# The order of the transfer queue where a quantised GLU kernel passes from its first batch to its second

## The chip, the cores and the metric

The kernel runs on one core of a Trainium2 chip. The metric is device microseconds (us) of one execution; less is better. The kernel before was timed in three runs: median 718.24 us, from 718.19 to 719.2.

## The reference

Four batches of 1024 tokens with 512 features go through one gated layer. The up weights are 4096 x 512, the down weights 512 x 2048.

```python
scale = cond @ norm_w.T + 1.0
h = x * (scale[:, None, :] * jax.lax.rsqrt(mean(x * x, axis=-1) + EPS))
val, gate = jnp.split(h @ up_w.T, 2, axis=-1)
h = val * jax.nn.gelu(gate, approximate=False)
hq = round(h * 127 / max|h|) / (127 / max|h|)             # per token
wq = clip(round(down_w / mean|down_w|), -1, 1) * mean|down_w|
y = hq @ wq.T + x
```

So `down_w` is reduced to a mean and to one of -1, 0, 1 per weight. The change concerns the transfers that bring `down_w` for that second step.

## The kernel before

**Tiles and slots.** The 2048 features of the value and of the gate are cut into 16 blocks of 128 (`NJ`). A batch has two halves of 512 tokens. One block of one batch is a slot, numbered g = 16 b + j; batch b = 1, the second, begins with slot 16. A slot multiplies by Winograd's scheme, with 7 products instead of 8. A product (`product`, L696) is 6 matmuls of 128 x 128 by 128 x 512 in fp16, in three terms of high and low parts. In the first batch only blocks 9 to 15 go that way; the earlier ones are done plainly (L711).

**Order in a slot.** `slot(g, ...)` writes this row on TensorE (PE), with PSUM banks A, B and E: `first` of g (bank A), `fourth` of g (E), `second` of g (B), `third` of the slot before (A of that slot), `fifth` of g (A), `gate` of the slot before (E), `value` of g (A). ScalarE (ACT) copies the bank between: `first_copy` (L803), `fourth_copy` (L811), `fifth_copy` (L818, it has to be done before `value` accumulates on the same bank), and it computes the two Gelus (L825, L842). VectorE (DVE) makes the sums and outputs.

**Weights.** A block has seven sums of its quarter weights, split in high and low fp16, at places 0 to 6 of a buffer in `SXY` or `S_more`. They are made in the first batch, written out to `s_dram` (`s_spill`, L469) and read back for the later batches (`s_load`): `s_load_x(g)` brings places 5 and 6 by a plain transfer (L485) and places 0 to 2 by a transposing one (L483), `s_load_y(g)` brings place 4 (L485) and place 3 (L483). `first` and `second` read places 5 and 6, `fourth`, `fifth` and `value` places 0, 1 and 2, and `gate` and `third` places 3 and 4. Slots 16 and 17 use the two blocks that are still on the core (`KEPT` = 2). Slot 18 is the first that needs loads, into the second buffer of `SXY`, which block 13 had. In slot j of the second batch `loads()` issues `s_load_x` for two slots ahead and `s_load_y` for one ahead.

**The signs of `down_w`.** They are made in eight parts n = 0 to 7 of 128 x 1024. `d_fetch(n)` (L542) loads a part, 512 KB, into one of three buffers by n modulo 3 (tags `xn`, `xt`, `nx`). On ACT `d_round(n)` (L546) and `d_sign(n)` (L553) turn it into signs in fp8, two parts to a tile `tn`. `d_turn(m)` (L556) is a transposing transfer of such a pair, m = 0 to 3, into `wd`. Fetch n + 3 needs `d_sign(n)` done; `d_turn(m)` needs `d_sign(2 m + 1)`. `D_LATE` places the ACT steps: parts 0 and 1 in slot 16, 2 and 3 in slot 17, 4 in slot 18, 5 and 6 in slot 19, 7 in slot 20. They are put between the Gelu at L825 and `fifth_copy`, or behind `fifth_copy`. DVE first reads `wd` in slot 25, at 258.2 us.

**The queue.** All these transfers are issued by SyncE (SP) in the order in which the code is written. SP carries out each row's waits before it goes on, so a row that waits holds up all rows behind it. The framework gives the transfers eight completion semaphores in turn: a row also waits until the transfer eight places ahead of it has landed. The string `FIRST_BATCH` is the written-out order of the first batch up to the last slots, and `D_MOVES` says which fetches and turns are issued in which slot j of the second batch. Before, they are passed to `s_load_x` as `between`, and so stand between its L485 and its L483.

Of the kernel before, what the change touches and what calls it, by code (L numbers as in the profile page):

```python
# [51 lines left out]
def glu_quant_kernel(  # L52
# [121 lines left out]
    def po_bank(name, shape=None):  # L174
        return bank("po", 3, shape, name)
# [313 lines left out]
    def s_load_x(g, between=()):  # L489
        s_load(g, *LOADS[0])  # L490
        for f in between:
            f()
        s_load(g, *LOADS[1])
# [15 lines left out]
    def d_at(n):  # L509

        return n // 4 + 2 * (n % 2), n // 2 % 2, n % 2
# [26 lines left out]
    def d_fetch(n):  # L538

        v = wpool.tile([P, HF], F32, name=f"dn_{n}", tag=("xn", "xt", "nx")[n % 3], bufs=1)  # L540
        c, u, _ = d_at(n)
        SP.dma_start(out=v, in_=down_w[c * P : (c + 1) * P, u * HF : (u + 1) * HF])  # L542
        dn[n] = v
# [189 lines left out]
    def gains(b):  # L733
        sg[b] = sm.tile([P, NJ, 2], F32, name=f"sg_{b}", tag="sg")
        DVE.tensor_scalar(sg[b], sw, dx[:, b : b + 1], None, ALU.mult)
# [509 lines left out]
    def second_part():  # L1245
# [18 lines left out]
        ((3, "y"), d_round, 6), ((3, "y"), d_sign, 6), ((4, "x"), d_round, 7), ((4, "x"), d_sign, 7),  # L1264
    ]
    D_MOVES = {
        0: ((d_turn, 0), (d_fetch, 3), (d_fetch, 4)), 1: ((d_turn, 1), (d_fetch, 5), (d_fetch, 6)),
        3: ((d_turn, 2), (d_fetch, 7)), 4: ((d_turn, 3),),
    }
    def second_slot():  # L1270
        w_turn(1)
        w_high(1)
        first_scale(4, ACT)
        first_scale(5, DVE)
        w_low(1)
# [80 lines left out]
    def take(steps):  # L1356
# [68 lines left out]
        gains slot.15.0 t_sum.3.0 s_spill.14.2 t_high.3.1 t_sum.3.1 slot.15.1 s_turn.15.0 s_high.15.1 t_low.3.0  # L1425
        t_turn.3.0 t_low.3.1 t_sum.3.2.1 s_low.15.1 max.5.1.1 slot.14.13 t_sum.3.3.1 t_high.3.2 t_turn.3.1
        slot.15.6 slot.14.14 s_spill.15.0 slot.14.8 s_turn.15.1 slot.15.7 t_low.3.2 slot.14.9 t_turn.3.2
        s_spill.13.1 slot.15.4 d_fetch.0 s_spill.15.2 slot.13.15 slot.14.11 slot.15.5 s_spill.8.2 max.6.1.0
        max.6.1.1 d_fetch.1 max.6.0.0 s_spill.6.2 max.6.0.1 d_fetch.2 slot.15.2 slot.15.3 slot.15.13 slot.14.12
        slot.15.14 s_spill.15.1 s_spill.14.1 slot.14.15  # L1430
    """

# [92 lines left out]
    for b in range(1, B):  # L1525
        dve, act = Filler(), Filler()
        if b > 1:
            gains(b)
        am = am_tile(b - 1)
        dq = state[b - 1] = sm.tile([P, 2 * NA], F32, name=f"dq_{b}", tag="dq")  # L1530
        if b == 1:
            for at, f, n in D_LATE:
                act.add(at, 1.1, lambda now, f=f, n=n: f(n))
        last_pair = NJ // 2 - 1
        for h in range(2):
            add_pair(
                dve, act, b - 1, last_pair, h, (0, "xz"[h]),
                lambda now, h=h: token_max(b - 1, h, am),
            )
        for h in range(2):  # L1540
            for cost, f in token_scale(h, am):
                dve.add((1, "x"), cost, lambda now, f=f: f())
        add_pieces(dve, act, b - 1, am, PIECES, (2, "x"))
        for i in range(NJ // 2 - 1):
            for h in range(2):
                add_pair(dve, act, b, i, h, (2 * i + 3, "x"))
        steps = {}
        pairs = {}
        if b + 1 < B:
            sc = []  # L1550
            steps[3, "z"] = [(lambda b=b, sc=sc: sc.append(cond_load_scale(b + 1)), (0, 0))]
            steps[5, "z"] = [(lambda b=b, sc=sc: cond_bring(b + 1, sc[0]), (0.4, 0))]
            p0 = b * NJ + 12
            plan = [
                (None, p0, ((6, "z"), (7, "x"), (7, "y"), (9, "y"), (10, "x"), (10, "z"))),
                (p0 + 4, None, ((9, "y"), (10, "x"), (10, "y"), (11, "y"), (12, "x"), (12, "x"))),
                (None, None, ((10, "y"), (11, "x"), (11, "y"), (13, "x"), (13, "y"), (13, "z"))),
                (p0 + 2, p0 + 4, ((9, "z"), (12, "x"), (12, "y"), (14, "x"), (14, "y"), (14, "z"))),
            ]
            for a, (at, nx_at, places) in enumerate(plan):  # L1560
                def make(a=a, at=at, nx_at=nx_at, b=b):
                    toks[a] = Tokens(b + 1, a, at, nx_at)
                    toks[a].load()
                fs = [
                    make,
                    lambda a=a: toks[a].norm(),
                    lambda a=a, sc=sc: toks[a].scale_and_sum(sc[0]),
                    lambda a=a: toks[a].high(),
                    lambda a=a: toks[a].low(DVE),
                    lambda a=a: toks[a].turn(),  # L1570
                ]
                costs = ((0, 0), (0, 1.6), (0, 1.5), (0, 2.1), (2.6, 0), (0, 0))
                for place, f, c in zip(places, fs, costs):
                    steps.setdefault(place, []).append((f, c))
        for j in range(NJ):
            g = b * NJ + j
            down = b + 1 < B and j in DOWN
            if down:
                pair, a = pairs[j], DOWN[j]
                xrs = [down_load(b - 1, h, a) for h in range(2)]  # L1580
            early_sums, late_sums = D_SUM_AT.get((b, j), ((), ()))
            left = SLOT_US + PAIR_US * down - OWN_US + 0.4
            more = D_SUM_US * len(late_sums) + 0.7 * (j + 1 == min(DOWN) and b + 1 < B)
            left -= D_SUM_US * len(early_sums) + more
            if b + 1 < B:
                left -= KEPT_US.get(j, 0)
            mine = {p: [sum(c[e] for _, c in steps.get((j, p), ())) for e in range(2)] for p in "xyz"}
            left -= sum(mine[p][0] for p in "xyz")
            act_left = {"x": 2.7, "y": 2.2 if down or b == 1 and j in (0, 1, 3, 4, 5, 6) else 1.1, "z": 0}

            def run(p):
                nonlocal left
                for f, _ in steps.get((j, p), ()):
                    f()
                if p == "x":
                    cap = min(left, 3.9 - 1.2 * (j in (1, 2)) - mine["x"][0] - (0 if down else mine["y"][0] + more))
                    left -= cap - dve.run((j, p), cap)
                elif p == "z":
                    left = dve.run((j, p), left)
                if p != "z":  # L1600
                    act.run((j, p), act_left[p] - mine[p][1])

            def early():
                if down:
                    pair.first([po_bank(f"po_{b}_{a}_{n}") for n in range(3)])
                    pair.sums(None, h_slots(g)[:, 0, 1])
                d_sums(early_sums)

            def next_pair():
                if b + 1 < B and j + 1 in DOWN:  # L1610
                    pairs[j + 1] = Pair(b - 1, DOWN[j + 1])
                    pairs[j + 1].sum1(h_slots(g + 1)[:, 0, 0])

            def more_sums():
                next_pair()
                d_sums(late_sums)

            mid = [nothing] * 3
            if j + 1 == min(DOWN):
                mid[0] = more_sums  # L1620
            if down:
                mid = [
                    lambda: (next_pair(), pair.third(xrs, dq), d_sums(late_sums)),
                    pair.fourth,
                    lambda: (loads(), pair.fifth()),
                ]

            def loads():
                if NJ + KEPT <= g + 2 < B * NJ:
                    moves = D_MOVES.get(j, ()) if b == 1 else ()  # L1630
                    s_load_x(
                        g + 2, [lambda f=f, n=n: f(n) for f, n in moves]
                    )
                if NJ + KEPT <= g + 1 < B * NJ:
                    s_load_y(g + 1)


            if b + 1 == B and j in DOWN and DOWN[j] < 3:
                pairs[DOWN[j]] = Pair(b - 1, DOWN[j])
                places = old_places(DOWN[j])  # L1640
                pairs[DOWN[j]].sum1(places[0])
                pairs[DOWN[j]].sums(*places[1:])
            if j == 4:
                token_turn(b - 1, am)
            if j == 5:
                bring_dq = token_undo(b - 1, dq)
            if j == 6:
                bring_dq()
            if j == NJ - 1:
                get_ready()  # L1650
            elif b == 1 and j == 0:
                get_ready()
            slot(g, lambda: run("x"), lambda: run("y"), lambda: run("z"), early, mid)
            if not down:
                loads()
        assert not act.items and not dve.items, (b, dve.items, act.items)


    b = B - 1
# [165 lines left out]
```

## Time and profile before

| what | value |
|---|---|
| median of three runs | 718.24 us (718.19 to 719.2) |
| the profiled execution's own time | 718.03 us |
| its span, first to last instruction | 716.1 us |
| PE busy in the span | 708.5 us (99%) |
| DVE, ACT, POOL busy | 590.4, 427.8, 144.9 us |
| granted TensorE clock | 0.999 |

Rows of the timeline give the start, the duration, the engine, the line, the operation and its tiles, and in square brackets how long the engine had been idle ahead of it and what ended that. Several instructions of a line are merged into one row. A matmul's end is modelled and overlaps the next start by about 0.17 us in rows that follow each other without idle time. The row of a transfer issue gives the time in which SP issued it, not when it landed; the transfers view gives the time from issue to landing, and only for some of the transfers.

### The profile page before, as it was taken

Reading aid. Unit: us, or ns where it says so; the run is one execution under the profiler, and the core shown is the slowest. Engines: PE = TensorE matmul, PEld = TensorE weight load, DVE = VectorE, ACT = ScalarE, POOL = GpSimd, SP = SyncE. Lnnn points to the kernel's source line nnn. Section 1 sums busy time; section 2 is a strip of 40 time slices with the busy share of each in tenths; the row PEclk is TensorE's granted clock in tenths of the full one; section 3 lists DMA queues with packets and bytes.
Section 4 is the critical chain, followed back from the end, with each engine's and each line's share of the span. In section 5 each row is a group of like instructions: output and inputs, shape, how many; then the busy total and the mean of one; then the engine's idle time right before and its main releaser. Section 6 shows DMA issues by size and latency. Waiting matters only on the chain.

```text
span 716.1 us, 10203 instructions
## 1 busy us (share of the span) xinstructions
PE 708.5 (99%) x3646; PEld 357.5 (50%) x3646; DVE 590.4 (82%) x877; ACT 427.8 (60%) x712; POOL 144.9 (20%) x152
## 2 busy tenths in 40 slices
PE   8999999999899999999999999999999999999998
PEld 4544444444344446664444445665444444445854
DVE  8999897798788789896798868876688888755896
ACT  6899877775767784544335676544334665332463
POOL 1753442221200305430100031450020000000120
PEclk9999999999999999999999999999999999999999
DMA  8999999999996656677646546785955454452253
GB/s 279 326 270 284 258 258 244 227 202 231 253 198 135 130 160 156 183 177 171 155 105 115 116 119 185 165 181 158 216 99 95 106 102 92 113 102 90 104 177 117
DMA packets 231860, 122.75 MB, mean 171 GB/s; under 512 B 193769, under 2 KB 202877, under 8 KB 231810
## 3 DMA queue, kind: packets, MB, share of 16 engines
q1 hardware_dynamic: 231658, 121.98, 69.3%
q8 instruction: 28, 0.46, 0.3%
q14 instruction: 22, 0.18, 0.1%
q10 hardware_dynamic: 152, 0.13, 0.1%
HBM read 52.71 MB, written 23.09 MB: 106 GB/s over the span
## 4 chain that ended last, share of the span: by engine, by line
PE 95%; DMA 2%; ACT 1%; SPq 1%; DVE 0%; issue 0%
PE A L696 38%; PE E L696 19%; PE B L696 10%; PE po L1060 9%; PE pg L711 6%; PE pv L711 6%; PE po_end L1012 4%; DMA SXY<-s_dram 1%; DMA dn<-in_L_cond_down_w_dram 1%; PE pz L1177 1%; PE ptx L1161 1%; PE pv L782 0%; PE po_B L1060 0%; PE pg L782 0%; SPq L469 0%; PE pw L382 0%
## 5 line engine op out<-in xcount | busy, mean ns | idle before, releaser
L696 PEld LDWEIGHTS <-SXY 128*128 128x128 f16 x2184 | 213.5, 98 | 251.9 <-DMA SXY<-s_dram 1.6
L696 PE MATMUL A<-R,SXY 128*128 128x512 f16 x1158 | 267.7, 379 | 0.0
L696 PE MATMUL E<-R,SXY 128*128 128x512 f16 x594 | 144.4, 379 | 1.1 <-DMA SXY<-s_dram 1.1
L831 DVE SCALAR_TENSOR_TENSOR H<-A,sg,t 128x512 f32<-128x512 f32 x55 | 41.2, 750 | 70.5 <-PE A L696 70.2
L983 DVE TENSOR_TENSOR H<-H,am 128x1024 f32<-128x1024 f32 x64 | 76.2, 1216 | 0.0
L696 PE MATMUL B<-R,SXY 128*128 128x512 f16 x312 | 75.8, 379 | 0.0
L842 ACT ACTIVATE t<-t,sg 128x512 f32<-128x512 f32 x55 | 39.6, 720 | 56.9 <-DVE t L839 56.8
L902 DVE TENSOR_REDUCE gm<-H 128x512 f32<-128x1024 f32 x56 | 69.0, 1233 | 1.0
L825 ACT ACTIVATE t<-B,sg 128x512 f32<-128x512 f32 x55 | 37.8, 687 | 40.2 <-PE B L696 40.0
L918 POOL PARTITION_ALL_REDUCE am<-R x8 | 14.3, 1793 | 228.4 <-DVE R L904 228.4
L818 ACT COPY t<-A 128x512 f32<-128x512 f32 x55 | 31.9, 580 | 38.3 <-PE A L696 35.8
L811 ACT COPY v<-E 128x512 f32<-128x512 f32 x55 | 32.2, 586 | 37.0 <-PE E L696 34.5
L803 ACT COPY B<-A 128x512 f32<-128x512 f32 x55 | 31.4, 572 | 35.3 <-PE A L696 34.6
L1060 PE MATMUL po<-wd,R 128*128 128x256 fp8e4 x416 | 52.4, 273 | 0.0
L851 DVE SCALAR_TENSOR_TENSOR H<-v,sg,t 128x512 f32<-128x512 f32 x55 | 43.1, 784 | 6.9 <-ACT t L842 6.9
L1060 PEld LDWEIGHTS <-R 128*128 128x128 bf16 (+1 forms) x448 | 43.8, 98 | 8.9
L848 DVE TENSOR_TENSOR v<-A,v 128x512 f32<-128x512 f32 x55 | 37.6, 684 | 12.3 <-PE A L696 11.3
L839 DVE TENSOR_TENSOR t<-E,t 128x512 f32<-128x512 f32 x55 | 37.4, 680 | 8.3 <-PE E L696 8.2
L991 ACT ACTIVATE H<-H 128x1024 f32<-128x1024 f32 x38 | 39.9, 1050 | 5.2 <-DVE H L983 5.2
L571 POOL TENSOR_SCALAR ssq<-ssq 128x2 f32<-128x2 f32 x12 | 4.7, 392 | 187.9 <-ACT xt L601 138.6
L904 DVE TENSOR_TENSOR R<-R,gm 128x512 f32<-128x512 f32 x56 | 41.1, 733 | 1.2
L995 ACT ACTIVATE R<-H 128x1024 bf16<-128x1024 f32 x38 | 40.1, 1056 | 1.2 <-ACT H L991 0.4
(235 smaller groups left out, 956.7 us busy)
## 6 DMA issues: line engine op xcount, KB each, us to landing
SXY<-s_dram SPq DMA_DIRECT2D x46, 256.0 KB, 3.2
H<-in_L_cond_up_w_dram SPq DMA_DIRECT2D x13, 512.0 KB, 5.7
SXY<-s_dram SPq DMA_DIRECT2D x46, 128.0 KB, 3.1
s_dram<-SXY SPq DMA_DIRECT2D x13, 384.0 KB, 4.6
xr<-in_x_dram SPq DMA_DIRECT2D x19, 256.0 KB, 3.0
out_dram<-xr SPq DMA_DIRECT2D x19, 256.0 KB, 2.4
H<-in_x_dram SPq DMA_DIRECT2D x8, 512.0 KB, 6.5
R<-in_L_cond_down_w_dram SPq DMA_DIRECT2D x8, 512.0 KB, 4.5
```

Of the source, the lines that this page charges most:

```text
L696: PE.matmul(o, s[:, w, k, :], operand(g // NJ, c, l, k), start=start and n == 0, stop=stop and n == len(TERMS) - 1, skip_group_check=True,)
L711: PE.matmul(ps, a[k // 2][:, w, k % 2, :], XP[:, l, k, h * TOK : (h + 1) * TOK], start=n == 0, stop=n == len(terms) - 1,)
L825: ACT.activation(self.t1, self.B, AF.Gelu, scale=gain(self.g, 1))
L831: DVE.scalar_tensor_tensor(h_half(self.g, 0), self.A, gain(self.g, 0), self.t1, ALU.mult, ALU.mult)
L842: ACT.activation(self.t2, self.t2, AF.Gelu, scale=gain(self.g, 1))
L851: DVE.scalar_tensor_tensor(h_half(self.g, 1), self.v, gain(self.g, 0), self.t2, ALU.mult, ALU.mult)
L902: DVE.tensor_reduce(gm[0], v, AX.X, ALU.max, apply_absolute_value=True)
L904: return [largest, lambda: DVE.tensor_tensor(m, m, gm[0], ALU.max)]
L983: DVE.tensor_tensor(v, v, r.to_broadcast([P, 2, TOK]), ALU.mult)
L991: ACT.activation(v, v, AF.Copy, bias=MAGIC)
L995: ACT.activation(q, by_tile(v), AF.Copy, bias=-MAGIC)
L1060: PE.matmul(po, w[:, j], m, start=start and j == 0, stop=stop and j == n - 1, skip_group_check=True,)
```

## The change

Two things move, both on SP alone. First, in `FIRST_BATCH`, fetch 0 goes ahead of a write-out of block 13 (`s_spill.13.1`), fetch 1 ahead of a write-out of block 15, and fetch 2 ahead of one of block 6. Second, in the second batch only one fetch is left between the two parts of `s_load_x` (fetch 3 in slot 16, fetch 6 in slot 18, by the new table `D_FIRST`); the turns and the other fetches are issued behind `s_load_x` and `s_load_y` of their slot, and fetches 6 and 7 change slots.

```diff
     D_MOVES = {
-        0: ((d_turn, 0), (d_fetch, 3), (d_fetch, 4)), 1: ((d_turn, 1), (d_fetch, 5), (d_fetch, 6)),
-        3: ((d_turn, 2), (d_fetch, 7)), 4: ((d_turn, 3),),
+        0: ((d_turn, 0), (d_fetch, 4)), 1: ((d_turn, 1), (d_fetch, 5)), 2: ((d_fetch, 7),),
+        3: ((d_turn, 2),), 4: ((d_turn, 3),),
     }
+    D_FIRST = {0: 3, 2: 6}
...
-        s_spill.13.1 slot.15.4 d_fetch.0 s_spill.15.2 slot.13.15 slot.14.11 slot.15.5 s_spill.8.2 max.6.1.0
-        max.6.1.1 d_fetch.1 max.6.0.0 s_spill.6.2 max.6.0.1 d_fetch.2 slot.15.2 slot.15.3 slot.15.13 slot.14.12
+        d_fetch.0 s_spill.13.1 d_fetch.1 s_spill.15.2 slot.15.4 slot.13.15 slot.14.11 slot.15.5 s_spill.8.2
+        d_fetch.2 max.6.1.0 max.6.1.1 max.6.0.0 s_spill.6.2 max.6.0.1 slot.15.2 slot.15.3 slot.15.13 slot.14.12
...
             def loads():
                 if NJ + KEPT <= g + 2 < B * NJ:
-                    moves = D_MOVES.get(j, ()) if b == 1 else ()
-                    s_load_x(
-                        g + 2, [lambda f=f, n=n: f(n) for f, n in moves]
-                    )
+                    between = [lambda: d_fetch(D_FIRST[j])] if b == 1 and j in D_FIRST else ()
+                    s_load_x(g + 2, between)
                 if NJ + KEPT <= g + 1 < B * NJ:
                     s_load_y(g + 1)
-
+                for f, n in D_MOVES.get(j, ()) if b == 1 else ():
+                    f(n)
```

On SP at the end of the first batch the difference reads as follows (- before, + now). `dn_0` to `dn_2` are the buffers of fetches 0 to 2; `s_dram<-SXY`, `<-s_rows` and `<-R` are write-outs; the first `s_dram<-SXY` is that of block 13.

```order
 L671 DMA_TRANSPOSE R_78<-nx_1_0_761 128x16x128
-L469 DMA s_dram_84<-SXY_81 128x1536
-L542 DMA dn_0_1798<-in_L0_cond_down_w_dram 128x1024
+L542 DMA dn_0_1791<-in_L0_cond_down_w_dram 128x1024
+L469 DMA s_dram_84<-SXY_81 128x1536
+L542 DMA dn_1_1794<-in_L0_cond_down_w_dram 128x1024
 L469 DMA s_dram_84<-s_rows_15_1_1699 128x1024
 L469 DMA s_dram_84<-R_78 128x512
-L542 DMA dn_1_1809<-in_L0_cond_down_w_dram 128x1024
```

Fetch 0 has moved up by one row, fetch 1 by three rows (two of them smaller write-outs).

On SP in the first slots of the second batch the order before is this, from the first load for slot 18 on. `tn_0` is the pair of signs of parts 0 and 1, `tn_2` that of parts 2 and 3.

```order
L485 DMA SXY_81<-s_dram_84 128x1024
L556 DMA_TRANSPOSE wd_80<-tn_0_1878 128x8x128
L542 DMA dn_3_1912<-in_L0_cond_down_w_dram 128x1024
L542 DMA dn_4_1914<-in_L0_cond_down_w_dram 128x1024
L483 DMA_TRANSPOSE SXY_81<-s_dram_84 128x12x128
L485 DMA SXY_81<-s_dram_84 128x1024
L556 DMA_TRANSPOSE wd_80<-tn_2_1954 128x8x128
L542 DMA dn_5_1989<-in_L0_cond_down_w_dram 128x1024
```

And now, from the same load on:

```order
L485 DMA SXY_81<-s_dram_84 128x1024
L542 DMA dn_3_1911<-in_L0_cond_down_w_dram 128x1024
L483 DMA_TRANSPOSE SXY_81<-s_dram_84 128x12x128
L556 DMA_TRANSPOSE wd_80<-tn_0_1878 128x8x128
L542 DMA dn_4_1915<-in_L0_cond_down_w_dram 128x1024
L485 DMA SXY_81<-s_dram_84 128x1024
L483 DMA_TRANSPOSE SXY_81<-s_dram_84 128x12x128
L485 DMA SXY_81<-s_dram_84 128x512
L483 DMA_TRANSPOSE SXY_81<-s_dram_84 128x4x128
L556 DMA_TRANSPOSE wd_80<-tn_2_1954 128x8x128
L542 DMA dn_5_1992<-in_L0_cond_down_w_dram 128x1024
```

The transposing load of slot 18 (the first L483) has left `tn_0`'s turn and fetch 4 behind it and has only fetch 3 ahead; fetch 5 now stands behind all four loads that slot 17 issues. The rows on PE, ACT, DVE and POOL stand as before; only line and buffer numbers differ there.

## Prediction

> **What bounds the kernel now.** The first view read is the page: the span, the busy times, and the chain of work that ended last, whose shares by engine are the third row here.
>
> ```profile
> span 716.1 us, 10203 instructions
> PE 708.5 (99%) x3646; PEld 357.5 (50%) x3646; DVE 590.4 (82%) x877; ACT 427.8 (60%) x712; POOL 144.9 (20%) x152
> PE 95%; DMA 2%; ACT 1%; SPq 1%; DVE 0%; issue 0%
> ```
>
> TensorE (PE) sets the end. A reordering of transfers can only give back time in which PE stands still, 7.6 us in the whole span. The table by stage says where: each row has the window, its length, and the busy time of PE; the granted clock stands behind POOL, then the busy share of the transfer engines.
>
> ```profile
> 165.00:180.00 15.00, 14.89 (x69) 6.53 (x68) 11.94 (x15) 7.93 (x11) 1.54 (x2) 1.00 0.94 243
> 180.00:200.00 20.00, 18.31 (x85) 8.15 (x85) 15.12 (x21) 15.22 (x20) 3.59 (x2) 1.00 0.97 247
> 200.00:260.00 60.00, 60.00 (x280) 27.20 (x279) 49.66 (x61) 44.95 (x62) 6.59 (x8) 1.00 0.68 144
> ```
>
> Around the seam of the batches PE lacks 0.11 + 1.69 = 1.80 us, and behind 200 nothing. The clock is full in all three, so no throttle is at work. The timeline of PE shows that these are two stops:
>
> ```profile
> 178.43 1.46 PE L696 MATMUL E<-R,SXY 128*128 128x512 f16 x6
> 180.63 1.45 PE L696 MATMUL A<-R 128*128 128x512 f16 x6 [0.74 <-ACT t L818]
> ...
> 183.21 1.46 PE L696 MATMUL E<-R,SXY 128*128 128x512 f16 x6
> 184.51 1.46 PE L696 MATMUL B<-R,SXY 128*128 128x512 f16 x6
> ...
> 189.69 2.75 PE L696 MATMUL A<-R,SXY 128*128 128x512 f16 x12
> 193.51 1.47 PE L696 MATMUL E<-R,SXY 128*128 128x512 f16 x6 [1.06 <-DMA SXY<-s_dram]
> ```
>
> The first stop is ahead of `value` of slot 16, which waits for ACT's `fifth_copy`; the second is ahead of `fourth` of slot 18, which waits for a load of summed weights. In brackets is the idle time by modelled ends, but a product that nothing holds up starts 1.30 us after the one before (183.21 to 184.51), before the 1.46 us of its row are over. So a stop costs what lies between the starts: 180.63 - 178.43 - 1.30 = 0.90, and 193.51 - 189.69 - 2.59 = 1.23 (2.59 for two products: 2.75 less the same overlap of 0.16). Together 2.13 us. That is the most that the change can give back.
>
> **The first stop.** ACT's timeline in slot 16 shows why the copy was late:
>
> ```profile
> 176.10 0.69 ACT L825 ACTIVATE t<-B,sg 128x512 f32<-128x512 f32 x1
> 177.78 1.15 ACT L546 ACTIVATE dn<-dn,wsc 128x1024 f32<-128x1024 f32 x1 [0.98 <-DMA dn<-in_L_cond_down_w_dram]
> 178.96 1.15 ACT L553 ACTIVATE tn<-dn,unmagic 128x1024 fp8e4<-128x1024 f32 x1
> 180.01 0.56 ACT L818 COPY t<-A 128x512 f32<-128x512 f32 x1
> ...
> 181.80 1.15 ACT L553 ACTIVATE tn<-dn,unmagic 128x1024 fp8e4<-128x1024 f32 x1
> ```
>
> ACT was free at 176.80 and stood until 177.78 for fetch 0. From that start it takes 180.63 - 177.78 = 2.85 us through round, sign and copy until PE can go. PE was ready at 178.43 + 1.30 = 179.73, so the round must start by 176.88: fetch 0 has to land 0.90 us sooner. When was it issued? SyncE's rows, in order:
>
> ```profile
> 168.66 2.00 SPq L671 DMA_TRANSPOSE R<-nx  x1
> 170.71 0.97 SPq L469 DMA_DIRECT2D s_dram<-SXY  x1
> 171.73 0.43 SPq L542 DMA_DIRECT2D dn<-in_L_cond_down_w_dram  x1
> ...
> 173.39 0.45 SPq L542 DMA_DIRECT2D dn<-in_L_cond_down_w_dram  x1
> ...
> 177.77 0.34 SPq L485 DMA_DIRECT2D SXY<-s_dram  x1
> 182.97 2.09 SPq L556 DMA_TRANSPOSE wd<-tn  x1
> 185.11 1.05 SPq L542 DMA_DIRECT2D dn<-in_L_cond_down_w_dram  x2
> 186.20 1.67 SPq L483 DMA_TRANSPOSE SXY<-s_dram  x1
> ```
>
> and what the transfers took from issue to landing: fetch 0, a 384 KB write-out, the first load of slot 18, and, from the chain, fetch 1 and the transposing load of slot 18:
>
> ```profile
> dn<-in_L_cond_down_w_dram SPq DMA_DIRECT2D x1, 512.0 KB, 6.0
> ...
> s_dram<-SXY SPq DMA_DIRECT2D x1, 384.0 KB, 8.0
> ...
> SXY<-s_dram SPq DMA_DIRECT2D x1, 256.0 KB, 7.6
> ...
> 173.39 7.20 DMA dn<-in_L_cond_down_w_dram
> ...
> 186.20 7.26 DMA SXY<-s_dram
> ```
>
> Fetch 0 now takes the place of the write-out at 170.71, 1.02 us sooner. With the same 6.0 us it lands at 176.7, and ACT goes on without a wait. 1.02 covers the 0.90, with 0.12 to spare. The worst end is that the landing doesn't move, since the transfer engines are 0.94 busy there: then 0.90 stays. The best is that it gains more than 1.02, because it no longer queues behind 384 KB; that buys nothing further, since ACT's Gelu ends at 176.79. I take the whole 0.90, the value at its own row's landing time. [...]
>
> Fetch 1 moves from 173.39 to about 170.71 + 0.43 + 0.97 + two gaps of 0.05 = 172.2. With at most 7.2 us (its landing was not what ACT waited for; ACT was busy until 180.57) it is there at 179.4, and the second round can start behind the copy, at about 179.6. Were it as late as before, the copy into bank B of slot 17 would lose about 0.4 us; that belongs to the same rival.
>
> **The second stop.** In the rows above the transposing load of slot 18 goes out at 186.20 because the turn of the first pair stands ahead of it and waits for ACT's second sign (181.80 + 1.15 = 182.95), takes SyncE 2.09 us, and two fetches follow. Now only fetch 3 is ahead. It needs the first sign, which ends at 178.96 + 1.15 - 0.98 = 179.1, so fetch 3 goes out near 179.2 and the load near 179.9. The load for places 5 and 6 ahead of them waited till 177.77 for fetch 0, eight places ahead; now it waits for the write-out of block 13, issued at about 171.2. With the 8.0 us of the longest write-out that is 179.2, so nothing moves by more than that. From 179.9 the transposing load takes 7.26 us, with less in the queue ahead of it than before: it lands by 187.2. PE wants it at 189.69 + 2.59 - 0.90 = 191.4. Four us are to spare, and 1.23 is gained. Even if all of the first stop stays, fetch 3 waits until 180.1, the load lands by 188.2, and this term holds.
>
> **What comes next.** PE behind 193.51 runs 2.13 us sooner, so each transfer and each step of ACT is due 2.13 sooner. The write-outs that fall behind a fetch or two (0.43 to 0.45 us of SyncE each) are of blocks read from slot 22 on, or free buffers used after 187; nothing. The turns go behind loads at no cost: DVE touches their result at 258. Fetch 4 gets earlier. Fetch 5 is the one that gets later, and with it I looked at the slot in which it is used:
>
> ```profile
> 191.76 1.24 SPq L556 DMA_TRANSPOSE wd<-tn  x1
> 193.35 0.83 SPq L542 DMA_DIRECT2D dn<-in_L_cond_down_w_dram  x2
> 194.29 2.13 SPq L483 DMA_TRANSPOSE SXY<-s_dram  x1
> 196.47 0.57 SPq L485 DMA_DIRECT2D SXY<-s_dram  x1
> 197.09 2.48 SPq L483 DMA_TRANSPOSE SXY<-s_dram  x1
> ...
> 206.02 1.14 ACT L546 ACTIVATE dn<-dn,wsc 128x1024 f32<-128x1024 f32 x1
> ...
> 208.72 1.15 ACT L546 ACTIVATE dn<-dn,wsc 128x1024 f32<-128x1024 f32 x1
> ...
> 209.06 2.75 PE L696 MATMUL A<-R,SXY 128*128 128x512 f16 x12
> ```
>
> It went out at 193.35. Now SyncE first waits for `value` of slot 17 to end (189.69 + 1.46 - 0.90 = 190.25), then issues 2.13 + 0.57 + 2.48 + 1.24 of loads and turn, some 6.6 us with gaps, so fetch 5 leaves at 196.9 and lands with 6.0 at 202.9. It is due at 206.02 - 2.13 = 203.9, and ACT has 209.06 - 206.02 - 2.85 = 0.19 us more. 1.2 us are to spare; the cost is nothing unless it takes over 7.2 us. Fetch 6 follows at about 198 and is due 2.7 us after fetch 5; fetch 7 has longer.
>
> **The sum.** Span: 716.1 - 0.90 - 1.23 = 714.0. The profiled execution took 718.03, so 715.9 by its own clock. The median of the runs is 0.21 above that execution; on the median it is 718.24 - 2.13 = 716.1.
>
> **The rivals.** *The first stop stays*, in part or whole: the transfer engines are saturated, fetch 0 or 1 does not land sooner, and only the second stop goes. For it: the busy share of 0.94 and the margin of 0.12. Against: the queue ahead of the fetch is shorter. The time is 718.24 - 1.23 = 717.0 if all of it stays; half of it gives 716.6. Chance 0.10.
>
> *Fetch 5 becomes the wait, and the kernel slower.* Place: `d_round(5)` in slot 19, ahead of `fifth_copy`, for which PE waits as in slot 16. Every us that the landing exceeds 7.2 costs PE a us. At 8.0, the longest landing quoted, PE loses 0.8 and the time is 716.9. Slower than before begins at 7.2 + 2.13 = 9.3 us; slower by over 0.2% at 10.8, and 11 us would give 719.9. For it: the issue durations of 2.13 and 2.48 show a queue that pushes back there. Against: no landing of a fetch above 7.2 us is in the trace. Chance 0.09, of which 0.04 is on the slow side.
>
> *The change does less than it says*: the load of slot 18 is still late, held by the write-out of block 13 that it now waits for, or another transfer takes PE's time. [...] It decides only if the load leaves after 184.1 (191.4 - 7.26), almost 13 us after the write-out's issue. With only the first stop gone it is 718.24 - 0.90 = 717.3, with nothing gained 718.2. Chance 0.07.
>
> **How the numbers follow.** The forecast, both stops gone, has 0.74: 716.1 us. A measurement can tell about 0.2%, 1.44 us, from no change. All of the forecast but 0.03 for scatter, and half of the first rival (0.05), are faster by more: 0.76. Slower has 0.04 from fetch 5. The rest, 0.20, is within. The range: at the low end the profiled execution's own 715.9 less 0.2 of scatter between executions, 715.7; at the high end it takes in the first rival whole and the milder half of fetch 5, 717.1. That holds the forecast's 0.74, 0.10 and 0.05; the sign of these cases is the same.
>
> **What would show it.** Right: ACT's first round starts at about 176.7 with no wait for `dn`, PE has no idle time ahead of `value` of slot 16, the transposing load of slot 18 leaves near 180, and the window 165 to 200 has full PE. Wrong: a wait for `dn` ahead of L546 at slot 16 or 19, or for `SXY<-s_dram` on PE in slots 18 to 20; or all steps as said and a span that has not shrunk by 2, which would mean that PE lost the time further on, in the tail behind 660.

## The result, and the profile after

The changed kernel took 716.91 us in the median of ten runs (716.35 to 717.35), the kernel before 718.6 in ten runs beside it (718.09 to 719.97). The ratio is 0.9974, with a 95% interval of 0.9964 to 0.9983: about 1.9 us faster, from 1.2 to 2.6. The profiled execution took 716.82 us with a span of 715.0.

The table by stage of the changed kernel has PE full where 1.80 us were missing:

```profile
165.00:180.00 15.00, 15.00 (x71) 6.66 (x69) 11.92 (x16) 8.54 (x13) 1.90 (x2) 1.00 0.98 244
180.00:200.00 20.00, 20.00 (x95) 9.06 (x93) 16.39 (x23) 15.33 (x21) 3.60 (x2) 1.00 1.04 252
```

Its timeline of PE has no bracket at either place; `value` of slot 16 is the row at 180.74, `fourth` of slot 18 that at 192.40:

```profile
179.45 1.46 PE L696 MATMUL E<-R,SXY 128*128 128x512 f16 x6
180.74 1.46 PE L696 MATMUL A<-R 128*128 128x512 f16 x6
...
189.81 2.75 PE L696 MATMUL A<-R,SXY 128*128 128x512 f16 x12
192.40 1.46 PE L696 MATMUL E<-R,SXY 128*128 128x512 f16 x6
```

180.74 - 179.45 = 1.29 and 192.40 - 189.81 = 2.59: the starts follow at full pace. On ACT the first round now stands right behind the Gelu:

```profile
177.12 0.69 ACT L825 ACTIVATE t<-B,sg 128x512 f32<-128x512 f32 x1
177.70 1.14 ACT L546 ACTIVATE dn<-dn,wsc 128x1024 f32<-128x1024 f32 x1
...
204.90 1.14 ACT L546 ACTIVATE dn<-dn,wsc 128x1024 f32<-128x1024 f32 x1
```

The second of these rounds is that of part 5 in slot 19; it has no wait for its fetch either. And on SyncE fetch 0 follows the tokens' last transfer, and the transposing load of slot 18 leaves at 180.50, ahead of the turn; the last row is fetch 5:

```profile
169.61 2.21 SPq L671 DMA_TRANSPOSE R<-nx  x1
171.87 0.81 SPq L542 DMA_DIRECT2D dn<-in_L_cond_down_w_dram  x1
...
178.29 0.34 SPq L485 DMA_DIRECT2D SXY<-s_dram  x1
180.06 0.34 SPq L542 DMA_DIRECT2D dn<-in_L_cond_down_w_dram  x1
180.50 2.02 SPq L483 DMA_TRANSPOSE SXY<-s_dram  x1
182.76 5.32 SPq L556 DMA_TRANSPOSE wd<-tn  x1
...
196.04 0.58 SPq L542 DMA_DIRECT2D dn<-in_L_cond_down_w_dram  x1
```

Why then is the span only 1.1 us shorter? Because this execution lost time at its start, where the two programs are the same. The first transposes on PE, in the kernel before and in the changed one:

```profile
9.70 2.14 PE L1161 MATMUL ptx<-ident,H 128*128 128x128 f32 x16 [0.16 <-ACT H L1154]
```

```profile
10.56 2.15 PE L1161 MATMUL ptx<-ident,H 128*128 128x128 f32 x16 [0.71 <-ACT H L1154]
```

They are 0.86 apart, and at 168, ahead of the seam, the same product starts 0.96 later (168.96 against 168.00). To compare the seam alone I add up, from PE's timelines between 168 and 214, by how much each start comes later than the matmuls ahead of it need (0.216 us each, 1.295 a product). The sum, called the seam below, is 2.21 us before and 0.13 after: 2.08 gained. Less the 0.96 lost ahead of it that is 1.12, the 1.1 by which the span is shorter.

### The profile page after: what moved, and what is told of

It is laid out like the page before. It is cut to its first block, busy times and chain, and to the rows that moved or that the text cites. A ratio compares the mean times of both kernels' runs of the same rounds, so it can differ in the third digit from the quotient of the medians.

```text
span 715.0 us, 10208 instructions
## 1 busy us (share of the span) xinstructions
PE 708.6 (99%) x3646; PEld 357.5 (50%) x3646; DVE 589.3 (82%) x877; ACT 428.5 (60%) x712; POOL 145.2 (20%) x152
## 4 chain that ended last, share of the span: by engine, by line
PE 98%; DMA 1%; ACT 0%; SPq 0%; DVE 0%; issue 0%; ACTq 0%
PE A L696 40%; PE E L696 20%; PE B L696 10%; PE po L1060 9%; PE pg L711 6%; PE pv L711 6%; PE po_end L1012 4%; DMA H<-in_x_dram 1%; PE ptx L1161 1%; PE pv L782 0%; PE po_B L1060 0%; PE pg L782 0%; PE pw L382 0%; PE po_A L1060 0%; PE po_E L1060 0%; ACT R L1127 0%
## 5 line engine op out<-in xcount | busy, mean ns | idle before, releaser
L851 DVE SCALAR_TENSOR_TENSOR H<-v,sg,t 128x512 f32<-128x512 f32 x55 | 43.9, 798 | 6.6 <-ACT t L842 6.6
L904 DVE TENSOR_TENSOR R<-R,gm 128x512 f32<-128x512 f32 x56 | 41.1, 733 | 1.2
```

The costliest lines, as they stand in the source:

```text
L851: DVE.scalar_tensor_tensor(h_half(self.g, 1), self.v, gain(self.g, 0), self.t2, ALU.mult, ALU.mult)
L904: return [largest, lambda: DVE.tensor_tensor(m, m, gm[0], ALU.max)]
```

## The experiments

All times are medians beside the kernel before on the same chip; a ratio has its 95% interval. The intervals are about 0.1% to each side, 0.7 us, so the parts of the change are told apart by the traces and the times only back them up.

**Only the first fetches** (`FIRST_BATCH` as changed, `D_MOVES` and `loads` as before).

> Only the fetches 0 to 2 move up; the second batch's order stays as before. Theory (two separate stops): the first stop goes (0.90 us), fetch 0 lands in time and ACT's round starts without a wait. The second stop stays: the transposing load of slot 18 still leaves behind the turn, which waits for the second sign, about 0.9 us sooner than before while PE wants it 0.9 us sooner as well; 1.1 to 1.3 us of it remain. Time about 0.9 us below before (ratio 0.9987). Rival (one cause, the crowded transfer engines): the two stops aren't separate, and this part alone gives either all 2.1 us (0.9970) or nothing (1.000).

Measured: 717.29 us, ratio 0.9986 (0.9977 to 0.9994). The seam is 1.04: no stop in slot 16, and 0.96 left ahead of `fourth` of slot 18, a little less than the 1.1 to 1.3 expected.

```profile
189.74 2.75 PE L696 MATMUL A<-R,SXY 128*128 128x512 f16 x12
193.29 1.47 PE L696 MATMUL E<-R,SXY 128*128 128x512 f16 x6 [0.80 <-DVE H L851]
```

The bracket names the DVE instruction that ended last (L851). `fourth` doesn't wait for it: in the changed kernel `fourth` starts at 192.40 and L851 only at 192.50. What it waits for is the load that it reads, which left behind the turn:

```profile
182.69 1.24 SPq L556 DMA_TRANSPOSE wd<-tn  x1
183.97 1.97 SPq L542 DMA_DIRECT2D dn<-in_L_cond_down_w_dram  x2
185.99 1.74 SPq L483 DMA_TRANSPOSE SXY<-s_dram  x1
```

185.99 + 7.26, the landing time it had before, is 193.25, and PE went on at 193.29. The two stops are separate, as the theory had it.

**Only the second batch** (`D_MOVES` and `loads` as changed, `FIRST_BATCH` as before), with one more execution of the same kernel.

> Only the order in the second batch changes; fetches 0 to 2 stay where they were. Theory: the first stop stays at about 0.90 us, with ACT waiting about 1 us for fetch 0; the second goes, 1.23 us, since the transposing load leaves near 181. Time about 1.2 us below before (ratio 0.9983). Rival (one cause): all or nothing, 0.9970 or 1.000.

> One more execution of the kernel with only the second batch's order changed, for its trace: in the first one fetch 0 landed 5.2 us after its issue instead of 6.0, and the first stop was 0.10 us instead of 0.90. Theory now (the stop depends on when fetch 0 lands in that execution): ACT's wait for fetch 0 and PE's stop ahead of value of slot 16 come out together, the stop 0.1 us shorter than the wait, somewhere between 0 and 0.9. Rival: the stop is 0.90 whatever ACT waits, or is gone for good in this order.

Measured: 717.71 us, ratio 0.9991 (0.9982 to 1.0), a smaller gain than expected, though 0.9983 is inside the interval. The second stop is gone in both traces. The first is there in both, in other sizes. ACT's round, and PE's `gate` and `value` behind it, in the first trace:

```profile
177.99 1.15 ACT L546 ACTIVATE dn<-dn,wsc 128x1024 f32<-128x1024 f32 x1 [0.19 <-DMA dn<-in_L_cond_down_w_dram]
```

```profile
179.44 1.46 PE L696 MATMUL E<-R,SXY 128*128 128x512 f16 x6
180.84 1.46 PE L696 MATMUL A<-R 128*128 128x512 f16 x6
```

and in the second:

```profile
178.58 1.15 ACT L546 ACTIVATE dn<-dn,wsc 128x1024 f32<-128x1024 f32 x1 [0.76 <-DMA dn<-in_L_cond_down_w_dram]
```

```profile
179.46 1.46 PE L696 MATMUL E<-R,SXY 128*128 128x512 f16 x6
181.43 1.46 PE L696 MATMUL A<-R 128*128 128x512 f16 x6 [0.51 <-ACT t L818]
```

By starts, PE lost 0.10 in the first and 0.67 in the second. Fetch 0 took 5.2 and 5.8 us to land, against 6.0 in the profiled execution before, where PE lost 0.90. So the stop is ACT's wait less about 0.1 (0.19, 0.76 and 0.98 against 0.10, 0.67 and 0.90), as the theory of the second execution says, and its size changes from execution to execution with one landing. The 0.90 of the prediction was one draw, the largest of three.

**Fetch 0 alone moved** (the changed kernel with fetches 1 and 2 at their old places; in the change fetch 1 goes ahead of two write-outs, so it moves up by two rows and not by three).

```diff
-        d_fetch.0 s_spill.13.1 d_fetch.1 s_spill.15.2 slot.15.4 slot.13.15 slot.14.11 slot.15.5 s_spill.8.2
-        d_fetch.2 max.6.1.0 max.6.1.1 max.6.0.0 s_spill.6.2 max.6.0.1 slot.15.2 slot.15.3 slot.15.13 slot.14.12
+        d_fetch.0 s_spill.13.1 slot.15.4 s_spill.15.2 slot.13.15 slot.14.11 slot.15.5 s_spill.8.2 max.6.1.0
+        max.6.1.1 d_fetch.1 max.6.0.0 s_spill.6.2 max.6.0.1 d_fetch.2 slot.15.2 slot.15.3 slot.15.13 slot.14.12
```

> The changed kernel, but of the first three fetches only fetch 0 moves up; fetches 1 and 2 stay at their old places. Theory: fetch 0 alone carries the first stop; same time as the changed kernel (0.9970 to 0.9974 of before), no idle time of PE ahead of value of slot 16, and at most 0.4 us ahead of second of slot 17 if fetch 1 comes late for the second round. Rival: fetch 1 is needed as well, ACT waits for it over half a us, and PE shows an idle time in slot 17.

Measured: 717.15 us, ratio 0.998 (0.9972 to 0.9989). The rival was right here. The stop in slot 16 is gone, but ACT waits for fetch 1, and the copy into bank B comes late:

```profile
179.95 0.56 ACT L818 COPY t<-A 128x512 f32<-128x512 f32 x1
181.75 1.15 ACT L546 ACTIVATE dn<-dn,wsc 128x1024 f32<-128x1024 f32 x1 [1.24 <-DMA dn<-in_L_cond_down_w_dram]
```

```profile
183.35 1.46 PE L696 MATMUL E<-R,SXY 128*128 128x512 f16 x6
185.23 1.46 PE L696 MATMUL B<-R,SXY 128*128 128x512 f16 x6 [0.42 <-ACT B L803]
```

185.23 - 183.35 - 1.30 = 0.58 us are lost ahead of `second` of slot 17. Of the first stop's 0.90, moving fetch 0 alone would have gained a third. In the trace before, fetch 1 landed at 173.39 + 7.20 = 180.59, just as ACT was done with the late copy (180.57), so that ACT's lateness covered it. What fetch 2 needs isn't told apart here.

**Fetch 5 late** (the changed kernel with fetch 5 behind the loads of slot 18).

```diff
-        0: ((d_turn, 0), (d_fetch, 4)), 1: ((d_turn, 1), (d_fetch, 5)), 2: ((d_fetch, 7),),
+        0: ((d_turn, 0), (d_fetch, 4)), 1: ((d_turn, 1),), 2: ((d_fetch, 5), (d_fetch, 7)),
```

> The changed kernel, but fetch 5 is issued only behind the loads of slot 18 instead of slot 17, some 8 us later, at about 204. Theory: ACT carries out its steps in order, so d_round(5) holds up fifth_copy of slot 19 and PE pays for each us of lateness: landing at 204 + 5.2 to 6 = 209.2 to 210, wanted at 204.9 + 0.19, so PE stops for 4.1 to 4.9 us ahead of value of slot 19, and the time is 721 to 722. Rival: ACT or PE has slack that the trace hides, or later slots make up for it; less than 2 us are lost.

Measured: 721.45 us, ratio 1.0042 (1.0028 to 1.0056): slower than before, by the mechanism of the prediction's rival. On ACT and on PE:

```profile
208.12 1.15 ACT L546 ACTIVATE dn<-dn,wsc 128x1024 f32<-128x1024 f32 x1 [3.93 <-DMA dn<-in_L_cond_down_w_dram]
```

```profile
205.82 1.46 PE L696 MATMUL E<-R,SXY 128*128 128x512 f16 x6
210.97 4.13 PE L696 MATMUL A<-R,SXY 128*128 128x512 f16 x12 [3.68 <-ACT t L818]
214.94 1.46 PE L696 MATMUL E<-R,SXY 128*128 128x512 f16 x6
```

The stop is 3.85 by starts, less than the 4.1 to 4.9 expected, and the twelve matmuls behind it take 3.97 from start to start instead of 2.59, 1.38 more. The table by stage says why: the granted clock, the column behind POOL, falls to 0.65.

```profile
211.00:215.00 4.00, 4.00 (x13) 1.51 (x13) 1.21 (x2) 2.73 (x3) 0.00 (x0) 0.65 0.02 4
```

Without these 1.38 us the time would have stayed below the 721 to 722 expected (716.91 + 3.85 = 720.8, an estimate), so the expected time came out partly by a cost that the expectation did not have.

Where the other traces have stops of 0.58 to 1.23 us ahead of 200, the clock is 1.00 in the window from 160 to 200, and behind the longest other stop, of 1.85 us in the run further on with fetch 0 still sooner, the products follow at 1.29 and 1.30 us from start to start. How long a stop has to be for the clock to fall is not shown.

**The turn ahead of the load, and both fetches ahead of it** (two kernels; in the first the turn and fetch 3 stand between the two loads of slot 18, the first of the two new lines, in the second fetches 3 and 4, the other; the turn or fetch 4 is taken out of `D_MOVES` accordingly).

```diff
-    D_FIRST = {0: 3, 2: 6}
+    D_FIRST = {0: ((d_turn, 0), (d_fetch, 3)), 2: ((d_fetch, 6),)}
+    D_FIRST = {0: ((d_fetch, 3), (d_fetch, 4)), 2: ((d_fetch, 6),)}
```

> The changed kernel, but the first turn stands again ahead of fetch 3 and of the transposing load of slot 18 (fetch 4 stays behind). Theory (what kept that load was the turn's wait for the second sign and its issue, not the traffic of the fetches): the load leaves behind the second sign (182.7 on the changed kernel's clock) and a turn's issue of 2.1 us and fetch 3, at about 185.5, and lands with 7.26 us at 192.8 against a need at 192.4: PE stops for about 0.4 us, more if the turn's issue takes longer than 2.1. Rival (the traffic of two fetches ahead of the load made the stop): no idle time of PE, same time as the changed kernel.

> The changed kernel, but fetches 3 and 4 both stand ahead of the transposing load of slot 18, the turn behind it. Fetch 4 needs the second sign too, so the load leaves only at about 183.5. Theory: it lands with 7.3 us at 190.8 against a need at 192.4; no idle time of PE, same time as the changed kernel. Rival (traffic): 1 MB ahead of the load delays it past 192.4, and PE stops in slot 18.

Measured: 717.12 us, 0.9978 (0.9969 to 0.9987), and 716.89 us, 0.9975 (0.9965 to 0.9985). Neither has a stop; the seams are 0.01 and 0.08. The second is as expected. In the first I had expected 0.4 us, with an issue of the turn of 2.1 us; it took 1.24, and the load left in time:

```profile
182.00 1.24 SPq L556 DMA_TRANSPOSE wd<-tn  x1
183.28 0.58 SPq L542 DMA_DIRECT2D dn<-in_L_cond_down_w_dram  x1
183.91 2.06 SPq L483 DMA_TRANSPOSE SXY<-s_dram  x1
```

183.91 + 7.26 is 191.2, and PE went on at 191.64. So this run doesn't tell the turn from the traffic: in these traces what counts is the moment at which the load leaves. Here it left 7.7 us ahead of the time at which `fourth` can start (191.64 - 183.91), in the kernel with both fetches 9.2 ahead. In the first experiment, with the turn and both fetches ahead of it, it left only 6.3 ahead (189.74 + 2.59 - 185.99), about 1 us less than the 7.26 that it took to land in the kernel before, and 0.96 was the stop.

**The copy ahead of the rounds** (the kernel before; on ACT in slot 16 `fifth_copy` goes first; `x` stands for the rounds and signs placed ahead of it, and `NJ` is 16).

```diff
-        x()
+        g != NJ and x()
         if up:
             cur.fifth()
-            cur.fifth_copy()
+            cur.fifth_copy(), g == NJ and x()
```

> The kernel before, with its queue untouched; only on ACT in slot 16 fifth_copy is put ahead of the rounds and signs of parts 0 and 1. Theory (ACT's time in slot 16 is used up, and its wait for fetch 0 is paid somewhere): the first stop goes, but the rounds begin at 179.1 instead of 177.8, the copy into bank B for slot 17 is ready at about 184.9 instead of 184.0, and PE stops for about 1.3 us ahead of second of slot 17; the turn waits for the second sign 0.8 us longer, and the second stop grows. 0.4 to 1.0 us slower than before. Rival (the wait for fetch 0 could be hidden by a better order on ACT): 0.9 us faster than before.

Measured: 718.99 us, ratio 1.0008 (0.9999 to 1.0017). The stop has moved instead of gone:

```profile
183.22 1.46 PE L696 MATMUL E<-R,SXY 128*128 128x512 f16 x6
185.71 1.45 PE L696 MATMUL B<-R,SXY 128*128 128x512 f16 x6 [1.04 <-ACT B L803]
...
190.89 2.75 PE L696 MATMUL A<-R,SXY 128*128 128x512 f16 x12
194.41 1.47 PE L696 MATMUL E<-R,SXY 128*128 128x512 f16 x6 [0.76 <-DMA SXY<-s_dram]
```

1.19 ahead of `second` of slot 17 and 0.93 at the second stop; the seam is 2.22, as before. The second stop did not grow as expected, since PE itself came later. So the rival falls for this order, which hides nothing. ACT shows where its cost lies:

```profile
179.53 0.59 ACT L818 COPY t<-A 128x512 f32<-128x512 f32 x1 [1.84 <-PE A L696]
180.02 1.15 ACT L546 ACTIVATE dn<-dn,wsc 128x1024 f32<-128x1024 f32 x1
```

ACT stands 1.84 us until PE has done `fifth`, and the round behind the copy has no wait for fetch 0 at all. So what is paid ahead of `second` of slot 17, 1.19 where 1.3 was expected, is this order's wait for PE; the theory had put it down to the wait for the fetch. That no order on ACT could hide the fetch isn't shown.

**Nothing ahead of the load; fetch 0 still sooner; fetch 6 behind** (three kernels around the changed one's limits). In the first `D_FIRST` has only slot 18's fetch 6, and fetch 3 stands first in slot 16's row of `D_MOVES`; in the third it has only fetch 3, and fetch 6 stands in `D_MOVES`. The three edits in turn:

```diff
-    D_FIRST = {0: 3, 2: 6}
+    D_FIRST = {2: 6}
```

```diff
-        slot.15.6 slot.14.14 s_spill.15.0 slot.14.8 s_turn.15.1 slot.15.7 t_low.3.2 slot.14.9 t_turn.3.2
-        d_fetch.0 s_spill.13.1 d_fetch.1 s_spill.15.2 slot.15.4 slot.13.15 slot.14.11 slot.15.5 s_spill.8.2
+        slot.15.6 slot.14.14 s_spill.15.0 slot.14.8 s_turn.15.1 slot.15.7 t_low.3.2 slot.14.9 d_fetch.0 t_turn.3.2
+        s_spill.13.1 d_fetch.1 s_spill.15.2 slot.15.4 slot.13.15 slot.14.11 slot.15.5 s_spill.8.2
```

```diff
-    D_FIRST = {0: 3, 2: 6}
+    D_FIRST = {0: 3}
```

> The changed kernel, but fetch 3 goes behind the transposing load of slot 18 as well, so that nothing stands between the two loads of slot 18. Theory: the load has some 4 us of slack in the changed kernel, so leaving earlier buys nothing, and fetch 3 still lands before 189.5; same time as the changed kernel. Rival: fetch 3 lands late for its round in slot 17, and PE stops ahead of value of slot 17 or second of slot 18.

> The changed kernel, but fetch 0 moves up one more row, ahead of the last transposing transfer of the second batch's tokens. Theory (the row behind that transfer is as early as fetch 0 can go): those tokens land at 169.61 + 4.4 = 174.0 in the changed kernel and fourth of slot 16 wants them at 174.27, so 0.26 us are to spare; a fetch's issue of 0.43 to 0.81 and its 512 KB in the queue ahead of them cost PE 0.2 to 2.4 us there, and nothing is gained, since fetch 0 already lands in time. Time between the changed kernel's and 2.4 us above it. Rival (the first stop is still there in part in most executions): up to 0.5 us faster than the changed kernel.

> One more execution of the kernel with fetch 0 ahead of the tokens' last transfer, for its trace: the profiled execution of the first run took six times as long as any other and shows nothing. Theory: PE stops ahead of fourth of slot 16 for 1 to 2.4 us, waiting for the transposing transfer into R, and has no stop ahead of value of slot 16; span about 1.6 us above that of the changed kernel. Rival: the time lies elsewhere, and fourth of slot 16 starts without a wait.

> The changed kernel, but fetch 6 goes behind the loads of slot 18 instead of between them; it then leaves at about 204.2 instead of 197.15. Theory: it lands at 209.4 to 210.2 and its round in slot 19 is due at 207.60; the round stands behind fifth_copy, so the late round and sign hold the next copy into bank B (210.73 in the changed kernel) by about 2 us, and PE stops for 1 to 2 us ahead of second of slot 20. Time 1 to 2 us above the changed kernel. Rival: the copy into bank B has more slack than that, nothing is lost.

Measured: the first kernel took 716.46 us, ratio 0.9971 (0.9959 to 0.9982), seam 0.03: not to be told from the changed kernel, as expected. The transposing load of the next slot, 19, of the same shape, took 6.8 us to land in the kernel before and 3.9 in the changed one, so the 7.26 used above is no constant either. The second kernel: 718.53 us, ratio 1.0002 (0.9993 to 1.0011), so the change's whole gain is lost (one execution of it took 4310 us and is left out of the ratio). The trace of one more execution names the place, `fourth` of slot 16, which waits for the tokens:

```profile
173.04 1.46 PE L696 MATMUL A<-R 128*128 128x512 f16 x6
176.19 1.46 PE L696 MATMUL E<-R 128*128 128x512 f16 x6 [1.70 <-DMA R<-nx]
```

1.85 us by starts, inside the 0.2 to 2.4. So the place behind that transfer is the earliest that costs nothing for fetch 0. The third kernel: 717.18 us, ratio 0.9988 (0.9979 to 0.9997). Fetch 6 landed at 208.8, ACT waited 1.36, and PE stopped for 0.70 ahead of `second` of slot 20, less than the 1 to 2 expected:

```profile
210.33 1.46 PE L696 MATMUL E<-R,SXY 128*128 128x512 f16 x6
212.33 1.46 PE L696 MATMUL B<-R,SXY 128*128 128x512 f16 x6 [0.54 <-ACT B L803]
```

That is what fetch 6 between the loads of slot 18 is for.

## Why the prediction was right, and where it was off

- *The whole is a matter of two stops of PE*: right. Both are gone in the trace after, PE waits for nothing from 30 to 660, and the seam gives 2.08 of the 2.13 in the sum.
- *The first stop, 0.90, from fetch 0 by way of ACT*: right in mechanism: the stop follows ACT's wait for fetch 0 in all three traces with the old place, and in all eight with the new one ACT has no wait. It was mis-sized as a typical value: the three have 0.90, 0.67 and 0.10. I took the one landing of 6.0 us for a constant where I had only that one. The margin of 0.12 had some luck too. Against PE's clock, which runs 1.02 us later there (179.45 against 178.43), fetch 0 left 0.88 sooner and not 1.02; with 6.0 us to its landing ACT would still have waited for up to 0.2 us. It landed within 177.70 - 171.87 = 5.83.
- *Fetch 1 is there in time and belongs to a rival*: the place was right, the weight wrong. Its move is needed; without it 0.58 comes back, not about 0.4.
- *The second stop, 1.23, from the queue ahead of the load*: right, and it is the sum of waits and issues ahead of it. I put the load's departure at 179.9 on the old clock; it was 180.50 on one that runs about 1 us later. The four us to spare were there too: it left 11.9 us ahead of `fourth` (192.40 - 180.50), and 7.7 ahead still cost nothing.
- *The write-out of block 13, a rival*: it played no part. It landed 5.5 us after its issue, and the load for places 5 and 6 left at 178.29. The 8.0 us of a write-out against the 6.0 of a read, in the rows that the prediction shows, are one row of each. By the medians on the page of the kernel before, write-outs of 384 KB took 4.6 us and reads of 512 KB 4.5 to 6.5, which doesn't show that write-outs land later.
- *Fetch 5 gets later and stays in time*: right, with no wait on ACT in slot 19 (the round at 204.90). The issues of 2.13 and 2.48 us, which the prediction read as a queue that pushes back, took 1.50 and 1.19 here (191.29 and 193.46); what held them in the kernel before is not shown. The rival built on it is real when the fetch is 7 us later, and dearer than a us for a us.
- *The total of 716.1*: measured 716.91, inside the range. By the time alone it is nearer to the first rival's 717.0; it is the traces, in which ACT doesn't wait for fetch 0, that decide for the forecast's mechanism. Against the median shown before (718.24) the ratio gives 716.4. The rest is the base: over more runs the kernel before has medians of 718.3 to 718.7, and its profiled execution had the earliest start of all thirteen traces (9.70, the others 9.90 to 11.03), so that execution had less loss at the start than the others and, by the three sizes of the first stop, perhaps more at the seam than is usual. How much of the gap between 2.13 and the measured 1.9 is the first stop's scatter and how much the measurement is not settled; the interval of 1.2 to 2.6 holds both.

## What to carry to other kernels

Where one queue carries transfers for several consumers, read for each the time at which it may leave at the latest, and order the queue by that; a row that waits for another engine should not stand ahead of one with a nearer date, unless its wait ends early enough for that date. Measure a stop from start to start, since the idle time counted from a matmul's modelled end understates it (0.74 against 0.90). And look at a landing time in more than one trace before it is made a term of a sum.

## What the hardware showed besides

In the kernel with fetch 5 late a stop of PE of 3.68 us cost another 1.38 us behind it, at a clock of 0.65 between 211 and 215; with stops of 0.58 to 1.23 us in four other traces the clock stayed at 1.00 between 160 and 200.

The issue of one and the same transposing turn took SyncE 1.24 to 5.74 us in these traces: 1.24 to 2.09 in the four in which the first turn stands ahead of slot 18's transposing load, 2.43 with a fetch between the two, and 3.09 to 5.74 in the eight in which it comes right behind that load (5.32 in the changed kernel). The second turn, right behind a smaller transposing load, took 1.24 or 1.25 in those eight. What holds it isn't settled. It did no harm, since the loads behind it are due late.

Two of the traces, fetch 0 alone and the first with only the second batch, have a further stop of 0.58 us at about 326, in slot 32, that none of the others has. DVE is late there, since some 20 us ahead of it the first of the two instructions below took 1.75 us in these traces and 0.68 or 0.69 in all others, and DVE had no idle time in between to make up for it. It stands here with POOL's work beside it, in the kernel with fetch 0 alone:

```profile
306.17 1.75 DVE L904 TENSOR_TENSOR R<-R,gm 128x512 f32<-128x512 f32 x1
307.85 1.75 DVE L1039 TENSOR_TENSOR H<-R 128x1024 bf16<-128x1024 bf16 x1
```

```profile
305.87 3.18 POOL L620 TENSOR_TENSOR H<-H,sc 128x512 f32<-128x512 f32 x2 [1.79 <-ACT H L619]
```

and in the changed kernel, where POOL starts later than the first of them:

```profile
304.89 0.69 DVE L904 TENSOR_TENSOR R<-R,gm 128x512 f32<-128x512 f32 x1
305.50 0.69 DVE L1039 TENSOR_TENSOR H<-R 128x1024 bf16<-128x1024 bf16 x1
```

```profile
305.27 3.28 POOL L620 TENSOR_TENSOR H<-H,sc 128x512 f32<-128x512 f32 x2 [2.19 <-ACT H L619]
```

L904 takes 0.68 or 0.69 where it starts 0.3 to 0.4 us ahead of POOL's instruction, and 1.75 in the two traces where it starts 0.3 behind it. (L1039 takes 1.75 or 1.76 in all traces but the changed kernel's, so it isn't what sets the two apart.) So the time of L904 goes with the order of the two starts in all thirteen traces. That of L1039 doesn't: it starts 0.23 behind POOL's instruction in the changed kernel as in the kernel before (306.62 against 306.39), and took 0.69 in the one and 1.76 in the other. Nothing was tried on this, and the cause is not shown. In the two traces it comes with 0.6 us of scatter in a kernel whose change is worth 2.
